# A second inner Strassen product (P4) in layer 1 of a two-layer graph attention kernel

## The chip, the cores and the metric

One core of one Trainium2 chip runs the whole program. The metric is device time in microseconds (us) of one execution. The kernel before takes 3223.03 us, the median of 3 runs (3222.26 to 3223.73). Every run here was in the fast state (granted TensorE clock 0.997 to 0.999 on the average). Chips and jobs differ by some microseconds (the medians of the kernel before lie between 3218.35 and 3221.52 us in the jobs below), so each kernel was timed in the same rounds as the kernel before.

Engines are named as in the profile: PE is TensorE, PEld its weight loads, DVE VectorE, ACT ScalarE, POOL GpSimd, SP SyncE, SPq the transfers that SyncE issued.

## The reference, cut to what matters

128 graphs of 128 nodes with 512 features go through two attention layers of 8 heads. Everything is fp32.

```python
# layer 0
Q, K, V = x @ W_q + b_q, x @ W_k + b_k, x @ W_v + b_v          # per graph 128x512 @ 512x512
attn = softmax(Q K^T / 8 + gate bias + log(adj + 1e-9));  x = attn V + x
# layer 1
q, k, v = x @ Wq.T + bq, x @ Wk.T + bk, x @ Wv.T + bv
attn = softmax(q k^T / 8 + log(clip(adj, 1e-8)));  out = (attn v) @ Wo.T + bo
x = layer_norm(x + out) * gamma + beta
```

## The kernel before

Four graphs make a group: 32 groups of layer 0 (t = 0 to 31), then 32 of layer 1 (t = 32 to 63). A group has the matrices v, q, k; from the second group of layer 1 on, k is followed by o of the group before. Each matrix (512 rows of four graphs by 512x512 weights) is done by Strassen's seven products P1 to P7 of half-size blocks; P2 in turn is done by seven products of 128x128 blocks, in four phases, each phase followed by additions on the vector engine. The products are laid out in seven slots per matrix. "b" means that the piece of the *previous* matrix stands in this matrix's slot.

```python
SLOTS = ("P1", "P2.1"), ("P4 b",), ("P3 b", "P2.2"), ("P6", "P2.3"), ("P5",), ("P7", "P2.4"), ()
PHASES = {"1": ("P1", "P2", "P5"), "2": ("P6",), "3": ("P7",), "4": ("P4", "P3")}

def matmul(dst, lhsT, rhs, start, stop):          # two halves of 64 array columns side by side
    for half in HALVES:
        nc.tensor.matmul(dst[half], lhsT[:, half], rhs, start=start, stop=stop, skip_group_check=True)

def inner(phase):                                  # one phase of P2
    v = t["t1"]
    if phase == "1": out_tile(); t["c"] = bank("p1")
    p, a, b = t["c"], Strassen.inner_weight(*t["W"]), t["B"]["inner"]
    for k, j in enumerate(Strassen.PHASES[phase]):
        ... matmul(p[:, at * N : (at + 1) * N], x, y, phase == "1" and k == 0, True)
    if phase == "1":   onto(v, 0, p, C21); add(0, 0, p, v, 0, 1)      # vector engine
    elif phase == "2": onto(v, C12, p, C21)
    elif phase == "3": onto(v, 3, p, C21); add(0, 0, p, v, 3, 4, C12 - 3)
    else:              add(0, 0, p, v, 1, 3); add(1, 1, t["b"], t["u3"])
```

PSUM banks: P1, P6, P7 and P4 of a matrix share p0 or p3, by turns; P5 and P3 use p2; the inner P2 uses p1. So a matrix's P1 takes the bank that the last but one matrix used. Each engine's queue gets its instructions in the order of the program. The parts of the schedule that the argument touches (a = slot 0 of the o that follows k of t, so a + 7 is slot 0 of v of t + 1; "pre" stands ahead of the slot's products, "post" behind them):

```python
put(pre,  a + 4 + step * k, scores, t, k)          # k = 0, 1: graphs (0, 1), (2, 3); then exp and the masked multiply
put(pre,  a + 7 + step * k, mix, t, (2 * k, 2 * k + 1))        # av products
put(post, a + 7 + step * k, normalise, t, k)
put(post, a + 8 + step * k, move, t, k, ...)       # 16 small DMAs o -> aT, which transposes by 32x32 blocks
put(post, a + 15, count, t)                        # two small vector operations on 128x32 and an accumulator read
put(post, first + ... + 7 * (b // 2) * late, load_graph, n, b, nc.sync)   # 4 DMAs of xT per graph
put(post, o + stored, store, t, k)                 # GpSimd: h*gamma, +beta; then the DMA of h (two buffers)
```

## Time and profile before

| view of the kernel before | value |
|---|---|
| TensorE busy, its share of the chain that ended last | 99%, 93% |
| period of a layer-0 group, of an undisturbed layer-1 group | 43.71, 55.56 us |
| outer product, inner product, start to start | 1.727, 0.218 us |
| layer-1 waits of TensorE for the store of h, sum | 3.5 us |
| vector engine's addition of a bank and an SBUF tile, 128x128, 128x256 (means of the groups) | 0.288 to 0.292, 0.425 to 0.426 us |

The prediction shows the lines and how they are read; two habits matter below. Ends of matmuls are modelled and overlap, so distances are taken from start to start. And a group of lines such as "x16" counts the trace's records, two for each fp32 matmul: an outer product, 8 matmul halves, shows as x16.

### The profile page before, as it was taken

The page shows a single profiled execution, that of the slowest core. Times are in us where ns is not written, and L with a number is a line of the kernel's source. Part 1 is how long each engine was busy: PE and PEld are TensorE (multiplying, and loading weights), DVE is VectorE, ACT ScalarE, POOL GpSimd, SP SyncE. Part 2 cuts the span into 40 slices and gives each one's busy share as a digit, 9 for nine tenths or more (in the row PEclk, how much of TensorE's full clock was granted, in tenths as well). Part 3 has the DMA queues.
Part 4 walks back from the last instruction along what each step waited for, and adds up shares of the span by engine and source line. Part 5 has one row for each costly group of instructions (what it writes and reads, how often), then busy time and mean ns, then how long its engine had stood idle before and what let it go on. Part 6 is the DMA issues. An engine that isn't in the chain of part 4 may idle for free.

```text
span 3215.3 us, 95438 instructions
## 1 busy us (share of the span) xinstructions
PE 3192.1 (99%) x39970; PEld 2371.2 (74%) x39970; DVE 1988.4 (62%) x4075; ACT 1132.9 (35%) x1949; POOL 1826.5 (57%) x1892
## 2 busy tenths in 40 slices
PE   9999999999999999999999999999999999999998
PEld 6777777777777777777777777777777777777775
DVE  6666666666666666675565555555565555555565
ACT  2333333333333333333333333333333333333332
POOL 4434433434433434475766767676766767676775
PEclk9999999999999999999999999999999999999999
DMA  5333333333333333342434334343433334343432
GB/s 126 84 80 83 78 83 70 83 80 84 79 84 67 84 82 83 92 112 55 93 72 78 89 75 94 72 98 67 91 75 77 89 75 95 72 99 66 90 75 76
DMA packets 1017246, 265.83 MB, mean 83 GB/s; under 512 B 942704, under 2 KB 949872, under 8 KB 1016816
## 3 DMA queue, kind: packets, MB, share of 16 engines
q1 hardware_dynamic: 1015728, 258.39, 36.0%
q8 instruction: 319, 5.23, 0.7%
q10 hardware_dynamic: 832, 1.05, 0.1%
q14 instruction: 111, 0.91, 0.1%
q0 software_dynamic: 256, 0.26, 0.0%
HBM read 159.92 MB, written 67.11 MB: 71 GB/s over the span
## 4 chain that ended last, share of the span: by engine, by line
PE 93%; SPq 3%; DMA 1%; POOL 1%; DVE 1%; issue 1%; ACT 0%; DVEq 0%; POOLq 0%; ACTq 0%
PE p3v L128 10%; PE p0q L128 9%; PE p3k L128 9%; PE s L128 8%; PE av L128 7%; PE p2v L128 7%; PE p2q L128 7%; PE p2k L128 6%; PE p0o L128 6%; PE p0k L128 4%; PE p3q L128 4%; PE p0v L128 3%; SPq L128 3%; PE p2o L128 3%; PE p1q L128 3%; PE p1v L128 3%
## 5 line engine op out<-in xcount | busy, mean ns | idle before, releaser
L128 POOL TENSOR_TENSOR xn<-o,xn 128x512 f32<-128x512 f32 x128 | 151.1, 1201 | 661.2 <-DVE o L128 423.3
L128 DVE TENSOR_TENSOR e<-e,adjT 128x1024 f32<-128x1024 f32 x256 | 419.0, 1677 | 139.4 <-ACT e L128 139.4
L128 POOL TENSOR_TENSOR xn<-xn,row 128x512 f32<-128x512 f32 x256 | 361.7, 1435 | 169.9 <-DVE gw L128 138.0
L128 PE MATMUL p0q<-T,wq 128*64 128x256 f32 x2256 | 267.5, 379 | 0.0
L128 PE MATMUL p3k<-T,wk 128*64 128x256 f32 x2256 | 267.5, 379 | 0.0
L128 PE MATMUL p3v<-wv,T 128*64 128x256 f32 x2256 | 267.4, 379 | 0.0
L128 PE MATMUL s<-qT,kT 64*128 64x128 f32 x4096 | 263.1, 278 | 0.0
L128 PE MATMUL av<-v,e 128*64 128x65 f32 x8192 | 262.0, 221 | 0.0
L128 PEld LDWEIGHTS av<-v,e 128*64 128x64 f32 x8192 | 257.8, 137 | 1.0 <-issue 0.8
L128 PEld LDWEIGHTS s<-qT,kT 64*128 64x128 f32 x4096 | 238.6, 188 | 22.6 <-issue 12.1
L128 POOL TENSOR_TENSOR h<-h,gamma 128x512 f32<-128x512 f32 x122 | 156.3, 1281 | 115.0 <-ACT h L128 115.0
L128 PEld LDWEIGHTS p3k<-T,wk 128*64 128x64 f32 x2256 | 159.5, 137 | 67.4
L128 PEld LDWEIGHTS p3v<-wv,T 128*64 128x64 f32 x2256 | 159.0, 137 | 67.6
L128 PEld LDWEIGHTS p0q<-T,wq 128*64 128x64 f32 x2256 | 159.4, 137 | 67.1
L128 POOL TENSOR_TENSOR T<-xT 128x512 f32<-128x512 f32 x128 | 193.9, 1515 | 18.0 <-DVE xT L128 14.4
L128 ACT COPY o<-av 128x520 f32<-128x520 f32 x256 | 151.8, 593 | 133.2 <-PE av L128 120.8
L128 POOL TENSOR_TENSOR h<-h,xn 128x512 f32<-128x512 f32 x124 | 157.7, 1303 | 43.2 <-ACT h L128 40.4
L128 DVE SCALAR_TENSOR_TENSOR gw<-xn,gw 128x512 f32<-128x512 f32 x256 | 177.4, 693 | 4.4
L128 DVE STREAM_TRANSPOSE xT<-xT 128x512 f32<-128x512 f32 x252 | 177.1, 703 | 0.7 <-issue 0.7
L128 PE MATMUL p0o<-wo,T_o 128*64 128x256 f32 x1488 | 176.6, 379 | 0.0
L128 DVE TENSOR_TENSOR t1q<-p1q,t1q 128x128 f32<-128x128 f32 x189 | 54.5, 288 | 180.2 <-PE p1q L128 180.2
L128 POOL TENSOR_TENSOR h<-h,beta 128x512 f32<-128x512 f32 x122 | 156.5, 1283 | 9.6
(231 smaller groups left out, 6559.1 us busy)
## 6 DMA issues: line engine op xcount, KB each, us to landing
x1d<-xn SPq DMA_DIRECT2D x64, 512.0 KB, 3.0
xT<-x1d SPq DMA_DIRECT2D x512, 64.0 KB, 2.5
xn<-x1d SPq DMA_DIRECT2D x64, 512.0 KB, 6.9
xT<-in_x_dram SPq DMA_DIRECT2D x496, 64.0 KB, 2.8
xn<-in_x_dram SPq DMA_DIRECT2D x62, 512.0 KB, 4.1
aT<-o SPq DMA_DIRECT2D x984, 32.0 KB, 2.0
out_dram<-h SPq DMA_DIRECT2D x60, 512.0 KB, 4.6
adjT<-in_adj_dram SPq DMA_DIRECT2D x256, 64.0 KB, 3.7
```

The source lines that it names most:

```text
L128: return lambda *args, **kw: self.tc.keep_in_program_order(f(*args, **kw))
```

## The change: its intent, and the diff

In layer 1 after its first group, P4 is also done by seven products of 128x128 blocks, for v, q, k and o: 123 matrices. That takes 8 matmul halves of 256 columns off and adds 14 of 128. P4's bank is shared with P1/P6/P7, so its four phases are scattered over the next matrix's slots. Since k's P4 now ends only in slot 4 of o, the scores of graphs 0 and 1, which read it, move one slot later, and their av products with them. SBUF is made free by smaller buffer counts; some work moves from GpSimd to the vector engine; the end of the last group is reordered.

```diff
-    SLOTS = ("P1", "P2.1"), ("P4 b",), ("P3 b", "P2.2"), ("P6", "P2.3"), ("P5",), ("P7", "P2.4"), ()
+    SLOTS = (
+        ("P1", "P4.1 b", "P2.1"), ("P4 b",), ("P3 b", "P4.2 b", "P2.2"), ("P6", "P4.3 b", "P2.3"), ("P5", "P4.4 b"),
+        ("P7", "P2.4"), (),
+    )
+    INSIDE = {t: ("P2", "P4") if t > NG else ("P2",) if t else () for t in range(LAST)}
+    INSIDE.update({("o", t): ("P2", "P4") if t > NG else () for t in range(NG, LAST)})
...
-        def inner(phase):
-            v = t["t1"]
+        def inner(i, phase):
+            m, v = (1, t["u3"]) if i == "P4" else (0, t["t1"])
...
+            if i == "P4" and i in inside:
+                return
...
-        nc.gpsimd.tensor_scalar_add(rs, MV[t][:, bs, 1], LN_EPS)
+        nc.vector.tensor_scalar_add(rs, MV[t][:, bs, 1], LN_EPS)
...
-            put(pre, a + 4 + step * k, scores, t, k)
+            put(pre, a + 4 + L * (1 - k) + step * k, scores, t, k)
...
-                put(pre, a + 7 + step * k, mix, t, (2 * k, 2 * k + 1))
+                m = a + 7 + L * (1 - k) + step * k
+                put(pre, m, mix, t, (2 * k, 2 * k + 1))
...
-            put(post, a + 15, count, t)
+            put(post, a + 17, count, t)
...  (last group: other order, other banks, sum and total of the count apart, last stores from SyncE and ScalarE by turns)
```

## The prediction

> **What bounds the kernel now.** I read the page first: the busy row, then the chain that ended last.
>
> ```profile
> PE 3192.1 (99%) x39970; PEld 2371.2 (74%) x39970; DVE 1988.4 (62%) x4075; ACT 1132.9 (35%) x1949; POOL 1826.5 (57%) x1892
> ...
> PE 93%; SPq 3%; DMA 1%; POOL 1%; DVE 1%; issue 1%; ACT 0%; DVEq 0%; POOLq 0%; ACTq 0%
> ```
>
> TensorE is the bound: 93% of the chain is its own work, and the clock row shows full speed in every slice. So the change is worth what it takes off TensorE, less what it makes TensorE wait. Next, the timeline of TensorE for 2500 to 2512 us, in layer 1 (start, length, group):
>
> ```profile
> 2503.66 1.90 PE L128 MATMUL p0o<-wo,T_o 128*64 128x256 f32 x16
> 2505.39 0.39 PE L128 MATMUL p1o<-wo,inner_o 128*64 128x128 f32 x4
> 2505.61 0.39 PE L128 MATMUL p1o<-woi,aT 128*64 128x128 f32 x4
> 2505.83 2.04 PE L128 MATMUL av<-v,e 128*64 128x65 f32 x64
> ```
>
> Read start to start, since modelled ends overlap. An outer product (x16) takes 2505.39 - 2503.66 = 1.73 us; one product of 128x128 blocks (x4) takes 0.22 us. Over the whole trace the medians of these differences are 1.727 us (1,338 outer products) and 0.218 us. A steady layer-1 group of four matrices repeats every 55.56 us, a layer-0 group every 43.71 us.
>
> Last, the timeline of all engines for 2047 to 2053 us, the worst TensorE wait of layer 1:
>
> ```profile
> 2047.23 1.59 SPq L128 DMA_DIRECT2D out_dram<-h  x1
> ...
> 2047.68 1.90 PE L128 MATMUL p3k<-T,wk 128*64 128x256 f32 x16
> ...
> 2047.97 0.29 DVE L128 TENSOR_TENSOR t1o<-p1o,t1o 128x128 f32<-128x128 f32 x1 [1.26 <-PE p1o L128]
> ...
> 2049.41 1.90 PE L128 MATMUL p2k<-xT,wk 128*64 128x256 f32 x16
> ...
> 2051.82 0.29 DVE L128 TENSOR_TENSOR h<-p1o,t1o 128x128 f32<-128x128 f32 x1 [3.56 <-DMA out_dram<-h]
> ...
> 2052.26 0.44 PE L128 MATMUL p1o<-woi,inner_o 128*64 128x128 f32 x4 [0.95 <-POOL T_o L128]
> ```
>
> The vector engine's first write of h waits for the previous group's store of the same buffer, 3.56 us; phase 2 of the inner P2 of o comes 0.44 us after that write starts. (The page names POOL, which had ended before; the write of h fits better.) Call w that wait of h. In all 8 groups with such a TensorE wait it equals w - 2.43, for w over 2.43 (w 2.96: 0.52 us; 2.64: 0.21), 3.5 us in total. The sum of w is the longest DMA wait of the vector engine:
>
> ```profile
> DVE h L128: 43.7, 24
> ```
>
> Why is the store late? SyncE's queue issues, without a gap, 16 aT, 8 xT, 16 aT, 8 xT and then the store, 33.2 to 35.4 us in all, and the store lands some 3.6 to 5.5 us later. The chain starts 0.32 us after TensorE's last read of aT (P3 of the previous o, in slot 2 of v).
>
> [...] 0.432 us for a pair of halves of 256 columns, 0.218 for 128; half the columns cost 50.5%. [...] an inner product ahead of the scores (128*64 to 64*128) takes 0.10 us more, 60 times in layer 1. Scores still follow inner products, so this stays. [...]
>
> **The change part by part.**
>
> 1. TensorE work. In layer 1 after its first group, v, q, k (31 groups) and o (30) get P4 inside: 93 + 30 = 123 matrices. The order listing confirms 984 outer halves fewer and 1,722 inner more, 8 and 14 per matrix. Each saves 1.727 - 7 x 0.218 = 0.201 us; 123 x 0.201 = **24.7 us** off the path. A group falls to 54.76 us.
>
> 2. Vector engine. Per matrix three partial sums and three adds more (0.29 us, 0.43 for 256 columns), for o four adds. Layer 1 gets 555 128x128 additions, 120 more for o and 93 of 256 columns: 675 x 0.29 + 93 x 0.43 = 236 us, and about 20 us of small scalings that leave POOL; some 8.2 us a group. It is busy 31 of 55 us now, then about 40: not the bound. ScalarE loses about 120 copies, beside the path.
>
> 3. POOL. Eight 128x128 sums (0.46 us) more per group, about six small operations (0.2) fewer: +2.4 us on 38 of 55. Beside the path.
>
> 4. Slack. P4 leaves slot 1, which is then empty. From phase 1 to phase 2 of the inner P2 TensorE has P4 + P3 = 3.45 us now; afterwards P3 and one inner P4 product, 1.945 us. Where the vector engine only needs 0.29 + 0.29 us this is enough (v, q, k). For o it has to fit h's wait too: TensorE will wait for w' - 0.93 instead of w - 2.43.
>
> 5. How w shifts. From the end of o's P3 to the end of P2 phase 1 of the next o, adding blocks up gives 36.2 us now (measured 36.2) and 37.3 after, because two P4 end pieces move behind. That helps by 1.1. But mix of k=0 moves to slot 1 of v, right ahead of that P3. After mix ends come the two copies (0.81 us), reciprocal (0.24) and scaling (1.37), so o is ready about 2.6 us after mix; P3 ends after 1.73. So the chain of aT starts about 0.9 instead of 0.32 us after P3. Net w' = w - 1.1 + 0.6 = w - 0.5. The sum of (w - 1.49) over the 30 groups, where positive, is 15 us, against 3.5 now: **+11.5 us**. A wait delays the next chain as much as the next o, so it does not wear off.
>
> 6. End of the last group. From the last mix of k=0 to TensorE's last large product: now 1.87 + 1.83 + 24.05 us; afterwards about 25.9, as P4 is split and the transposes get other banks (two waits for ScalarE's copies there, 0.7 and 1.1 us). The vector engine's tail after it stays at about 7 us, then 6 us to the end of the program. -1.5 us, 0.2 of it counted already: **-1.3**.
>
> 7. Start. Twenty small warming products instead of four; the first real product waits for weights (8.3 us) and the next for a copy behind a DMA on the vector engine. Nothing, within 0.3 us. Smaller buffer counts in the small pool and halves of qT and kT: their readers come long before. POOL's four extra weight sums at the layer change are beside the path.
>
> Sum: 3223.0 - 24.7 + 11.5 - 1.3 = 3208.5. I say **3207**: part 5 rests on tenths of a microsecond, and the two-sided error is longer downwards.
>
> **The rivals.**
>
> A. The whole gain arrives: no new waits, and the old 3.5 us go too. 3223.0 - 24.7 - 3.5 - 1.3 = 3193.5. For it: vector engine and POOL both have over a quarter of each group left, and v, q, k have no DMA in the loop. Against it: the 24 waits of h in 30 groups, and a slack cut by 1.5 us.
>
> B. My chosen one: the store of h takes part of the gain back, at 3203 to 3215.
>
> C. The store takes nearly all: if the chain starts 1.1 us later rather than 0.6, w' = w, and 27 us of waits against 3.5 leave 3223.0 - 24.7 + 23.8 - 1.3 = 3221.
>
> D. The vector engine becomes the bound. It would need 55 us a group against 40; its in-order queue can delay an inner phase behind two masked multiplies (1.6 us each), but scores come a slot from the phases that need it. Up to 5 us; over 3225 very unlikely.
>
> **Range and chances.** A is the low end, C the high: 3195 to 3217 should hold it 8 times in 10. Two per cent are 64 us; TensorE saves 25 at most, and no wait I see costs 64. Faster 0.01, same 0.97, slower 0.02.
>
> **What would show it right or wrong.** Part 1: the p0 and p3 groups with 128x128 shapes at 0.218 us from start to start. Part 4 and 5: waits of TensorE in p1o phase 2 behind p3k's or p0k's inner product, 10 to 20 us in all, each following a vector-engine wait for out_dram<-h of over 0.9 us; group periods of 54.8 plus 0 to 2 us. If the periods are 54.8 flat, A is right and my reading of the slack is wrong. Part 5: the first aT issue about 0.9 us after o's P3. Part 6: from the last outer TensorE product to the end still some 13 us. Wrong altogether if the granted clock falls, or if vector-engine lateness shows in v, q and k as well.

## The result, and the profile after

The changed kernel took 3227.38 us, the median of 6 runs (3225.94 to 3230.91); the kernel before in the same rounds 3221.52 (3219.43 to 3223.73). The ratio is 1.0019, with a 95% interval of 1.0007 to 1.0032. Ratios here are the mean time of one kernel's fast runs over that of the other's of the same rounds, so not quite the ratio of the medians. Within 2% it is "the same", but it is slower, and the 3207 us and the range up to 3217 were wrong.

The page of the changed kernel, busy row and chain:

```profile
PE 3191.9 (99%) x41478; PEld 2455.4 (76%) x41478; DVE 2267.1 (70%) x4970; ACT 1045.2 (32%) x1764; POOL 1913.9 (59%) x1968
...
PE 86%; SPq 6%; DVE 5%; DMA 2%; issue 1%; ACT 0%; POOL 0%; DVEq 0%; POOLq 0%; ACTq 0%
```

TensorE is busy for 99% as before, which tells nothing: its ends are modelled. The chain tells more. TensorE's own work has gone from 93% to 86%; DVE, 1% before, and SyncE's transfers have come in. Layer-0 periods are unchanged at 43.71 us, so the difference is in layer 1, where the prediction had 54.76 us a group and the shortest measured is 55.54. Adding up start-to-start distances of a whole group between fixed products shows three places that are longer than their products.

**Place one: k's P1, 0.34 us late in every group.** All engines of the changed kernel, end of q and start of k (start, length, engine, line, operation, tiles, and in brackets the idle time before it):

```profile
2149.87 1.28 POOL L135 TENSOR_TENSOR h<-h,gamma 128x512 f32<-128x512 f32 x1
...
2150.23 0.39 PE L135 MATMUL p3v<-wv1i,T 128*64 128x128 f32 x4
2150.27 0.90 DVE L135 TENSOR_SCALAR rs<-mv 128x2 f32<-128x2 f32 x1
2150.45 1.90 PE L135 MATMUL p0q<-T,wq 128*64 128x256 f32 x16
2151.09 0.17 DVE L135 TENSOR_SCALAR ok<-rc 128x32 f32<-128x32 f32 x1
2151.23 1.27 POOL L135 TENSOR_TENSOR h<-h,beta 128x512 f32<-128x512 f32 x1
2151.29 1.26 DVE L135 SCALAR_TENSOR_TENSOR ok<-rc,ok 128x32 f32<-128x32 f32 x1
...
2152.39 0.39 PE L135 MATMUL p1q<-xT,wq1i 128*64 128x128 f32 x4
...
2152.48 0.41 DVE L135 TENSOR_TENSOR v<-p3v,u3v 128x256 f32<-128x256 f32 x1
...
2152.95 0.87 PE L135 MATMUL p3k<-xT,wk 128*64 128x256 f32 x6 [0.17 <-DVE v L135]
```

v's P4 is complete in bank p3 at about 2150.5. The addition that reads it (v<-p3v,u3v) starts at 2152.48, because it stands in the vector engine's queue behind rs and the two operations of the count (ok). k's P1 reuses p3 and starts 0.56 us after q's last inner product instead of 0.22. It also takes 1.78 us itself, start to start, instead of 1.727 in all 30 groups, so 0.39 us a group; the expectation of count_early below reckons 30 x 0.39 = 11.7. Two small operations are very long: 0.90 us for two columns, 1.26 us for 32. Both end as GpSimd's operation ends. The count's second operation by itself, before and after (number, then shortest, median and longest in ns):

```profile
L128 DVE SCALAR_TENSOR_TENSOR ok<-rc,ok x64: 191/192/194, 81.2 to 3206.8; 128x32 f32<-128x32 f32 x64
```

```profile
L135 DVE SCALAR_TENSOR_TENSOR ok<-rc,ok x64: 191/391/1267, 84.2 to 3216.1; 128x32 f32<-128x32 f32 x64
```

In layer 1 of the changed kernel it is long in 30 of 31 cases, and in all 30 it ends 46 to 54 ns after the GpSimd operation during which it began. rs is alike: in 31 of 66 cases it takes 0.86 to 0.97 us and ends 23 to 27 ns after GpSimd's gamma (beta once), in the others 0.15 to 0.17. The additions of a bank and an SBUF tile are not held up: of 1,830 at 128x128 in this trace 803 begin inside a 128x512 operation of GpSimd, and none is longer than 0.30 us. What sets these operations apart, no view shows. The change moved the root (rs, LN_EPS added to the variance) onto the vector engine and the count two slots later, both beside GpSimd's gamma and beta.

**Place two: from P3 of o to the scores, 0.32 to 0.49 us too long in every group.** TensorE of the changed kernel there:

```profile
2183.57 2.01 PE L135 MATMUL p2o<-wo,aT 128*64 128x256 f32 x15
2185.30 0.38 PE L135 MATMUL p0o<-woi,innerP_o 128*64 128x128 f32 x2
2185.41 0.38 PE L135 MATMUL p2o<-wo,aT 128*64 128x256 f32 x1
2185.52 0.38 PE L135 MATMUL p1v<-wv1i,innerP 128*64 128x128 f32 x2
...
2188.32 0.38 PE L135 MATMUL s<-qT,kT 64*128 64x128 f32 x2
```

P3 (p2o) has 15 records, then two of the next product, then its sixteenth: the two halves of the array have got out of step, and one runs alone at the end of the stretch. Records overtake each other: the last of p2o, ahead of p0o in the program, starts at 2185.41, p0o at 2185.30. The stretch takes 4.75 us (2183.57 to 2188.32) instead of 1.727 + 0.436 + 1.727 + 0.436 + 0.10 = 4.43. The list of instructions with their waits names a suspect, the same in both kernels:

```
p2o<-wo,aT 64x256 [waits for 8 DMAs and DVE]      first half
p2o<-wo,aT 64x256 [waits for 8 DMAs]              second half
```

Fifteen of these 17 waits become eight instructions of their own in TensorE's queue, 51 ns long and some 0.1 us apart. In the kernel before they run from 2120.11 to 2120.93 in the profile, well inside P4 of o, and P3's first two halves start at 2122.039 and 2122.046. In the changed kernel av stands ahead of P3, with matmuls 28 ns apart; the eight run from 2183.01 to 2183.83. The four of the second half come last, two of them after the first half has started, at 2183.573, and the second half starts 0.31 us later. Ahead of this stretch, in most groups, v's inner P2 also waits (0.15 us) for the vector engine, which has two masked multiplies ahead of the additions of o, since the scores come a slot later; place two is this and the halves.

**Place three: the store of h**, as predicted. Waits of the changed kernel (engine, tile, who ended the wait: sum in us, times, longest):

```profile
DVE h L135 <- DMA out_dram<-h: 28.5, 23, 2.7
...
PE p1o L135 <- DVE h L135: 8.4, 10, 1.6
```

Counted from start to start, TensorE's waits here are 11.2 us in this profile.

This profile was the slowest of the six runs (3230.91 us). A later one of the same kernel (run after_again, span 3221.0, kernel before 3215.3) serves for the sum:

| part of the span | after less before, us |
|---|---|
| start and layer 0 | -0.8 |
| first two groups of layer 1, the av that moved out of them counted in | +1.1 |
| 29 groups: P4 inside | -22.8 |
| 29 groups: old waits for the store | -3.9 |
| 29 groups: place one 11.3; P3 of o to the scores 9.9; ahead of it 5.4; store of h 3.9; other 0.4 | +30.9 |
| last group and end, without the av that moved into it | +1.1 |
| sum | +5.6 |

The spans differ by 5.7 us. P4 does bring its part; the waits take it back.

### The profile page after: what moved, and what is told of

Same layout as the page of the kernel before. It is cut to its first block, busy times and chain, and to the rows that moved or that the text cites. A ratio compares the mean times of both kernels' runs of the same rounds, so it can differ in the third digit from the quotient of the medians.

```text
span 3228.8 us, 99418 instructions
## 1 busy us (share of the span) xinstructions
PE 3191.9 (99%) x41478; PEld 2455.4 (76%) x41478; DVE 2267.1 (70%) x4970; ACT 1045.2 (32%) x1764; POOL 1913.9 (59%) x1968
## 4 chain that ended last, share of the span: by engine, by line
PE 86%; SPq 6%; DVE 5%; DMA 2%; issue 1%; ACT 0%; POOL 0%; DVEq 0%; POOLq 0%; ACTq 0%
PE p3v L135 9%; PE p3k L135 8%; PE s L135 7%; PE p0q L135 7%; PE av L135 7%; PE p2v L135 7%; SPq L135 6%; PE p2k L135 6%; PE p0o L135 6%; PE p2q L135 5%; PE p0k L135 4%; PE p3q L135 4%; PE p0v L135 3%; PE p2o L135 3%; PE p1v L135 3%; PE p1k L135 3%
## 5 line engine op out<-in xcount | busy, mean ns | idle before, releaser
L135 POOL TENSOR_TENSOR xn<-xn,row 128x512 f32<-128x512 f32 x256 | 380.1, 1505 | 132.6 <-DVE gw L135 123.9
L135 PE MATMUL p3v<-wv,T 128*64 128x256 f32 (+1 forms) x2132 | 249.5, 361 | 0.5 <-DVE u3v L135 0.5
L135 PE MATMUL p3k<-T,wk 128*64 128x256 f32 (+1 forms) x2132 | 239.9, 360 | 0.0
L135 PE MATMUL p0q<-T,wq 128*64 128x256 f32 (+1 forms) x2132 | 239.6, 360 | 0.0
L135 PEld LDWEIGHTS p3k<-T,wk 128*64 128x64 f32 x2132 | 149.0, 137 | 57.7
L135 PEld LDWEIGHTS p0q<-T,wq 128*64 128x64 f32 x2132 | 148.1, 137 | 58.5
L135 ACT ACTIVATE e<-s 128x1024 f32<-128x1024 f32 x128 | 124.3, 1022 | 125.3 <-PE s L135 125.3
L135 PE MATMUL p0o<-wo,T_o 128*64 128x256 f32 (+1 forms) x1368 | 159.0, 354 | 0.8 <-DVE u3o L135 0.4
```

The lines of the kernel that those rows point to most:

```text
L135: return lambda *args, **kw: self.tc.keep_in_program_order(f(*args, **kw))
```

## The experiments

Theory: three independent causes, each an accident of position (the count beside GpSimd, av ahead of P3's semaphores, the store behind xT in SyncE's queue). Rivals: the vector engine has too much to do, whatever its order; or the rest of the change is what costs.

| run | median us (n) | range | before, same rounds | ratio (95% interval) |
|---|---|---|---|---|
| count_early | 3220.95 (13) | 3217.3 to 3227.5 | 3218.69 | 1.0010 (1.0002 to 1.0018) |
| mix_between | 3221.79 (13) | 3212.3 to 3227.6 | 3218.69 | 1.0012 (1.0004 to 1.0021) |
| store_first | 3218.41 (13) | 3216.7 to 3220.3 | 3218.69 | 1.0001 (0.9992 to 1.0009) |
| all_but_p4 (wrong results) | 3236.67 (5) | 3234.8 to 3239.3 | 3218.69 | 1.0059 (1.0045 to 1.0072) |
| after_again | 3224.84 (16) | 3222.5 to 3228.2 | 3218.35 | 1.0022 (1.0015 to 1.0030) |
| three_mended | 3191.56 (5) | 3190.7 to 3193.0 | 3218.35 | 0.9918 (0.9904 to 0.9931) |
| three_mended_old_end (wrong results) | 3191.03 (5) | 3189.8 to 3193.2 | 3218.35 | 0.9916 (0.9903 to 0.9930) |
| before_store_first | 3216.61 (13) | 3213.1 to 3218.6 | 3218.35 | 0.9992 (0.9984 to 1.0000) |
| store_first_touch | 3231.72 (5) | 3230.1 to 3233.7 | 3219.43 | 1.0038 (1.0024 to 1.0051) |
| store_first_gamma_later | 3211.09 (9) | 3209.7 to 3212.3 | 3219.43 | 0.9976 (0.9966 to 0.9985) |
| three_mended_xt | 3189.25 (4) | 3188.9 to 3189.5 | 3219.43 | 0.9906 (0.9891 to 0.9921) |
| two_mended | 3219.59 (13) | 3210.6 to 3223.1 | 3218.91 | 1.0000 (0.9991 to 1.0008) |

**count_early**, an edit of the changed kernel:

```diff
-            put(post, a + 17, count, t)
+            put(post, a + 15, count, t)
```

> One edit to the changed kernel: the layer-1 and layer-0 count (two small vector-engine operations on 128x32) goes back from the post of q's slot 3 to that of q's slot 1. Theory: its second operation, 0.19 us in the profile of before, takes 1.26 us in that of the changed kernel because it stands beside GpSimd's multiplications for the store [...]; the addition that reads v's P4 bank is queued behind it, and the first product of k, which reuses that bank, waits 0.34 us, in all 30 groups [...]. Expected: from q's last inner product to k's P1 0.22 us instead of 0.56, period 55.3 in undisturbed groups instead of 55.65, time 3227.4 - 11.7 = 3216 us. Rival: the vector engine simply has too much to do in that slot, and taking 0.4 us of work elsewhere only moves the wait: under 3 us of gain, the 0.56 stays above 0.4.

The wait is gone: 0.22 us from q's last inner product to k's P1 in all groups, the shortest period 55.14. The count's second operation takes 0.19 us in all 31 groups. But the time falls by only about 4 us against the changed kernel (1.0010 against 1.0022), not 11.7: TensorE's waits for the store of h are 11.8 us in this profile. The mechanism holds, the expected time does not.

**mix_between**: av of graphs 0 and 1 between P1 of v and P4 of o.

```diff
-                m = a + 7 + L * (1 - k) + step * k
-                put(pre, m, mix, t, (2 * k, 2 * k + 1))
+                between = t > NG and k == 0
+                m = a + 7 + (L * (1 - k) if not between else 0) + step * k
+                put(mid if between else pre, m, mix, t, (2 * k, 2 * k + 1))   # mid: behind the slot's first product
```

> One edit to the changed kernel: in layer 1 the av products of graphs 0 and 1 go between P1 of v and the inner P4 of o, instead of right ahead of P3 of o. Theory: the semaphores that P3 of o waits on (its two halves read what 16 DMAs brought) take some 0.1 us each in TensorE's queue; during the short av products (28 ns each) the queue is not far enough ahead, the second half of the array starts one matmul late, and the stretch from P3 of o to the scores takes 4.75 to 4.92 us instead of 4.43. Expected: that stretch at 4.43, P1 of v to P3 of o at 4.91 instead of mostly 5.06, together 0.45 us a group or 13 us; the chain of aT starts about 1.3 us earlier, which takes 5 to 8 us off the waits for the store of h. Time 3206 to 3214 us. Rival: the halves get out of step because of their own operands, wherever av stands: 4.75 stays and only the 5 to 8 us are gained, 3220 us.

The halves are in step in all groups: P3 of o is one piece of 16 records everywhere. TensorE of this run:

```profile
2120.82 0.61 PE L135 MATMUL p0o<-wo,T_o 128*64 128x128 f32 x8
...
2122.14 1.90 PE L135 MATMUL p2o<-wo,aT 128*64 128x256 f32 x16
2123.86 0.39 PE L135 MATMUL p0o<-woi,innerP_o 128*64 128x128 f32 x4
...
2126.56 0.71 PE L135 MATMUL s<-qT,kT 64*128 64x128 f32 x7
```

The stretch is 4.42 us here and 4.43 in most groups; in 6 it is 4.70 to 4.90 for another reason, which is shown under two_mended. From P1 of v to P3 of o it is 4.91 throughout. The expected 5 to 8 us off the store did not come, and again most of the gain is missing. The chain of aT starts 0.16 us after the vector engine has scaled o (0.48 once), and this scaling stands behind the additions of the slot: the chain starts 0.75 to 0.96 us after P3 in most groups, 0.80 to 0.88 in most of after_again, so an earlier av does not bring it forward.

**store_first**: the second half of the loads of xT two slots later, behind the store.

```diff
-                put(post, first + (-1 if t == 0 else 2 + 7 * (b // 2) * late), load_graph, n, b, nc.sync)
+                put(post, first + (-1 if t == 0 else 2 + 9 * (b // 2) * late), load_graph, n, b, nc.sync)
```

> One edit to the changed kernel: the last eight loads of xT (graphs 2 and 3) are issued two slots later, so that the store of graphs 0 and 1 stands ahead of them in SyncE's queue and is issued about 5.4 us earlier. Theory: the vector engine's first write of h waits for this store, and TensorE for that; the sum of TensorE's waits there is about 11 us in the profile of the changed kernel. Expected: no TensorE wait left between k's inner P4 and the second phase of o's inner P2 (0.22 us each), time 3227.4 - 11 = 3216 us. Rival: the store lands late because it is long in landing and not because it is issued late, or the loads of xT become the late ones: no gain, or a new wait of GpSimd's sums and TensorE at v's first product.

The waits are gone in all 30 groups: the vector engine's first write of h starts 0.03 us after the addition ahead of it (0.16 once). All periods lie between 55.40 and 55.71, and the runs spread over 3.6 us, against 10 to 15 in the two runs above and 5.7 in after_again: the store made the periods scatter, and part of the spread between runs. The gain is 6.4 us against after_again by the medians, not 11. The stretch of place two is 0.32 to 0.39 us too long a group in this run, which has no other wait there.

**all_but_p4**: P4 done whole, every other part of the change kept. The results are wrong, because the inner weights of P4 had still been written over the plain ones; the instructions and their order are those meant.

```diff
-    INSIDE = {t: ("P2", "P4") if t > NG else ("P2",) if t else () for t in range(LAST)}
-    INSIDE.update({("o", t): ("P2", "P4") if t > NG else () for t in range(NG, LAST)})
+    INSIDE = {t: ("P2",) if t else () for t in range(LAST)}
+    INSIDE.update({("o", t): ("P2",) if t > NG else () for t in range(NG, LAST)})
```

> The changed kernel with the seven products inside P2 alone, as before (and in the o matrices too); every other part of the change stays. Theory: the three waits of the changed kernel are made by P4 lying inside (no P4 addition of v for k's bank to wait on, an outer P4 of o between av and P3), so they go, and with them the 24.7 us of saving: periods of 55.56 plus the old waits for the store, time 3221.5 plus 2 to 5 us for the last group and the start of layer 1, 3223 to 3227. Rival: the other parts (later mix, later count, roots on the vector engine) cost some 30 us by themselves and P4 inside brings its 24.7 in full: 3250 us.

Neither. The period is 56.18 us, 0.62 above before. 0.58 of it is one wait: v's inner P2 behind P1 of v (2.30 us instead of 1.73), for the vector engine's additions of o (the view of waits has PE p1v behind DVE h 29 times), which stand behind the two masked multiplies of the scores that came a slot later. So the later scores, which P4 of k forces, cost by themselves (read from the trace; no run moved them alone); with P4 inside, its first phase stands in that place and hides most of it (0.15 us left). The waits of places one and two are not there, as expected.

**after_again**, the yardstick of the second job.

> The changed kernel unaltered, on the chip and in the rounds of the runs beside it, as their yardstick. Theory: slower than the kernel before by 0.1 to 0.3 per cent, spread over 5 to 10 us by the waits for the store of h, which differ from run to run. Rival: the first measurement was an accident of that chip, and the two are equal within 0.05 per cent.

The slowdown is confirmed on another chip: 1.0022.

**three_mended**: the three edits together.

> The changed kernel with all three edits: count early, av between P1 of v and P4 of o, store ahead of the second loads of xT. Theory: the three waits are all that stood between the change and its 24.7 us in layer 1, and the first two edits alone gave little because each shortens the group and the chain of 48 issues and the store of h, whose length is fixed, takes the time back; with the store moved as well they add up. Expected: periods of 54.75 to 54.85 us in every group of layer 1, no scatter; the time is that of the store-first run, 3218.4, less 30 x (0.39 + 0.32 + 0.15) = 26: 3193 us. Rival: TensorE is then ahead of something else (loads of xT, GpSimd's sums, masked multiplications), which takes half of it back: 3203 us or more, and a new wait with a name in the profile.

All periods of the groups 35 to 62 are 54.77 us; the prediction had said 54.76. The page:

```profile
PE 3167.0 (99%) x41478; PEld 2418.7 (76%) x41478; DVE 2231.7 (70%) x4970; ACT 1046.4 (33%) x1764; POOL 1913.7 (60%) x1968
...
PE 97%; DVE 1%; SPq 1%; DMA 0%; issue 0%; POOL 0%; ACT 0%; DVEq 0%; POOLq 0%
```

TensorE's own work is 97% of the chain, with the same number of vector operations as in the changed kernel: the vector engine at 70% is not too slow, it was late. The three edits bring 33.3 us together, 3.9, 3.1 and 6.4 alone (each against after_again, by medians; the single edits ran on another chip, where the kernel before took 3218.69 us instead of 3218.35).

**two_mended**: the first two edits, the store as in the change. It asks why the parts don't add up.

> The changed kernel with the count early and av between P1 of v and P4 of o, and the store where the change has it. Theory: these two take 25 us of TensorE's waits away (30 x 0.86), but the chain of 48 issues and the store of h is not shorter, and the vector engine's wait for the store grows by about what the group shrinks between the chain's start and the next o, 0.4 to 0.8 us; so TensorE's waits there come to 8 to 20 us, and the time to 3205 to 3217 us, spread over 8 us or more between runs. Rival: the three waits are independent, and what the two edits gave singly (3.9 and 3.1 us against the changed kernel in the same job or with the same kernel before) was chance of the chip: 3199 us, like the three together plus 7, with little spread.

Waits and chain of this run:

```profile
DVE h L135 <- DMA out_dram<-h: 50.0, 28, 3.2
...
PE p1o L135 <- DVE h L135: 20.6, 20, 2.1
```

```profile
PE 80%; SPq 10%; DMA 4%; DVE 3%; issue 1%; POOL 1%; ACT 0%; DVEq 0%; POOLq 0%; ACTq 0%
```

TensorE's waits for the store come to 28.2 us, more than I expected, and the median is 2.6 us above my range. From the chain's start to the end of P2's phase 1 of the next o there are 35.9 to 36.6 us here, 35.9 in the kernel before and mostly 37.25 in after_again; the chain of issues is 33 to 36 us in all three, and the store needs some 3.5 to 5.5 more. Whatever the first two edits save in this window, the store takes. The theory holds, the independence of the waits does not.

A fourth wait is in these traces. In 13 groups of this run, and in the 6 of mix_between, the stretch from P3 of o to the scores takes 4.48 to 4.90 us although the halves are in step. All engines of this run in one of them:

```profile
1621.45 3.49 POOL L135 TENSOR_TENSOR xn<-xn,row 128x512 f32<-128x512 f32 x2
1621.65 2.15 DVE L135 TENSOR_TENSOR o<-o,rc 128x1024 f32<-128x1024 f32 x1
...
1624.33 0.27 DVE L135 TENSOR_TENSOR u3o<-p0o,u3o 128x128 f32<-128x128 f32 x1
...
1624.66 0.44 PE L135 MATMUL p0o<-wo,T_o 128*64 128x128 f32 x4
```

The scaling of o, 1.23 us at its shortest, begins inside an addition of GpSimd; in all 15 groups where it takes 1.69 us or more it ends 1.08 us after that addition. The addition u3o of the inner P4 stands behind it, and TensorE's p0o waits for u3o. This takes 3.2 us in this run and 2.2 in mix_between. It also delays the chain of aT, which starts 0.16 us after the scaling: 1.2 to 1.8 us after P3 in these 15 groups, 0.75 to 0.96 in most others. In three_mended the scaling takes 1.34 to 1.41 us in every group. No run moved GpSimd's addition alone, so this is read from the traces and not tried.

**store_first_touch**: two matmuls of one column ahead of v's inner P2 take over P3's 16 waits for DMAs; av stays ahead of P3.

```diff
+        for half in HALVES:
+            nc.tensor.matmul(p[half, 0:1], aT[:, 2, 2, half], aT[:, 2, 2, 0:1], start=True, stop=True, ...)
```

> The store-first kernel (3218.4 us) with two matmuls of one column each ahead of the inner P2 of v, which read the half of aT that P3 of o needs; av stays right ahead of P3. They take over the 16 waits for DMAs of P3 (8 on each half of the array), so P3 waits for one semaphore alone. Theory: the halves get out of step because those 16 waits stand between the first matmuls of P3's two halves, and av is too short to hide them; so without the waits the stretch from P3 of o to the scores takes 4.43 us instead of 4.75, though av has not moved: 30 x 0.32 = 10 us less, at most 0.1 us a group given back by the extra matmuls: 3208 to 3211 us. Rival: it is av ahead of P3 itself (its mixed order of halves, its waits for the masked multiplications) that puts the halves out of step: 4.75 stays, and the extra matmuls add to 3218 to 3222 us.

The halves are in step in all groups, 4.43 us, though av has not moved: the semaphores are the cause. The time is a miss: the new matmuls have the same waits and hide them no better behind inner products. They take 0.75 us a group, and P1 of v to P3 of o grows from 5.06 to 5.83 us. The waits moved, and cost more there.

**store_first_gamma_later**: the count stays in q's slot 3; ScalarE's scaling of h and GpSimd's gamma and beta come two slots later (and the loads of xT with them, behind the store).

```diff
-                    stat, scaled, end, stored = (((5, 6), 6, 9, 10), ((9, 10), 10, 13, 14))[k]
+                    stat, scaled, end, stored = (((5, 6), 6, 11, 12), ((9, 10), 10, 13, 14))[k]
```

> The store-first kernel (3218.4 us) with the count where the change put it, in q's slot 3, and the scaling of graphs 0 and 1 of h on ScalarE and their multiplication and addition on GpSimd two slots later (the loads of xT behind that store again). Theory: the count's second operation is slow (1.26 us) only because GpSimd is in a multiplication when it comes; with GpSimd at rest there it takes 0.19 us, v's addition starts on time, and k's P1 follows q's last product after 0.22 to 0.3 us instead of 0.56, with as many vector operations ahead of it as ever: 7 to 11 us less, 3207 to 3212 us. Rival: it is the number of vector operations queued ahead of that addition: 0.56 stays, time within 2 us of 3218.4.

All engines of this run, same place as in place one:

```profile
2138.97 0.17 DVE L135 TENSOR_SCALAR rs<-mv 128x2 f32<-128x2 f32 x1
2139.05 0.17 DVE L135 TENSOR_SCALAR ok<-rc 128x32 f32<-128x32 f32 x1
...
2139.26 0.20 DVE L135 SCALAR_TENSOR_TENSOR ok<-rc,ok 128x32 f32<-128x32 f32 x1
...
2139.39 0.41 DVE L135 TENSOR_TENSOR v<-p3v,u3v 128x256 f32<-128x256 f32 x1
2139.88 1.28 POOL L135 TENSOR_TENSOR h<-h,gamma 128x512 f32<-128x512 f32 x1
...
2141.02 0.39 PE L135 MATMUL p1q<-xT,wq1i 128*64 128x128 f32 x4
...
2141.24 1.25 PE L135 MATMUL p3k<-xT,wk 128*64 128x256 f32 x10
```

The same root and count stand ahead of v's addition, and take 0.17 and 0.20 us with gamma and beta out of the way. GpSimd is not quite at rest: its power of 128x2 (0.69 us in the record) begins some 0.04 us before the count's second operation in all 30 groups and does not hold it up (0.20 us in all 30). k's P1 follows after 0.22 us. It is gamma and beta, not the number of operations. Of the 11 us that place one costs, 5.0 arrive in the groups of this profile, since k's products lose 0.2 us a group elsewhere. Another 2.8 us come from the second group of layer 1 (60.8 us in store_first, 58.0 here), whose loads of xT the edit also put later; so the time of 3211 us, though in the expected range, is not place one alone.

**before_store_first**: the store edit on the kernel before.

> The kernel before with the one edit to the order of the loads of xT and the store of h. Theory: its waits for the store (3.5 us in its profile, those of 2.43 us and more of the vector engine) go, and with them most of the scatter between runs: 3 to 4 us faster than before, runs within 4 us of each other. Rival: the scatter and the waits have another source (the load of natural x, the clock): no difference over 1 us.

The profile has no store wait left (periods 55.56 and 55.57, 3.9 us less), but the time falls only by 1.7 us. In that profile the first o of layer 1 waits longer for its transposed input (3.3 us instead of 1.2), and the granted clock fell to 0.5 for 3.4 us right behind this wait: 65.2 us against 61.0 for that group. Whether the edit or that run made the wait longer was not tried apart. The runs spread over 5.5 us, not within the expected 4 (8.1 for the kernel before).

**three_mended_old_end**: the last group's end as before (wrong in four graphs, since P4 of that o is done whole with overwritten weights).

> As the run before it, and the last group's end in the order of the kernel before (its P4 of o done whole, the graphs 0 and 1 of the last group but one first, all last stores from SyncE). The results of four graphs of 128 are wrong on purpose: P4 done whole reads weights that the inner P4 has overwritten. Theory: from the first product of the last v to the end takes 97 to 98 us with the changed order and 94.5 before; some 1.5 us of the excess are the change's order on the vector engine after the last product, and the rest waits of the new order, so the old order brings 2 to 3 us: 3190 to 3191 us, the stretch 94 to 95 us. Rival: the excess is only the three waits in the last group (0.86 us) and the later scores, which stay: within 1 us of the run before.

The medians differ by 0.5 us, within both intervals. From the first product of the last v to the end the profiles have 96.5 us, 96.8 in three_mended and 94.5 in the kernel before; 94 to 95 were expected. The rival holds: going back to the old order gains next to nothing.

**three_mended_xt**: in the second group of layer 1 also, the loads of xT behind the chain of aT.

```diff
-                put(post, first + (-1 if t == 0 else 2 + 9 * (b // 2) * late), load_graph, n, b, nc.sync)
+                put(post, first + (-1 if t == 0 else 2 + (12 if t == NG + 1 else 9) * (b // 2) * late), load_graph, n, b, nc.sync)
```

> The kernel with the three edits (3191.6 us) and, in the first group of layer 1 that has one, the second eight loads of xT behind the second chain of aT. Theory: what TensorE still waits for once, 2.1 us at the first o of layer 1 (its vector addition stands behind a turn of aT that waits for its DMAs), is the issue of that chain, 5.4 us of which is xT; so the second group's period falls from 60.1 to 58 us, time 3189.5 us. Rival: the chain's landing is set by its bytes or by av, not by the issue, or GpSimd's sums become the limit: less than 0.7 us gained.

The group takes 58.01 us, as expected. This version computes the right result and is the fastest: 3189.25 us, 0.9906 of the kernel before.

## Why the prediction was wrong

- **Part 1 (24.7 us saved by TensorE)** was right. three_mended has 54.77 us a group, predicted 54.76; before_store_first 55.56, both without waits.
- **Part 2 (vector engine busy about 40 of 55 us, not the bound)** was right as a share and led to the wrong conclusion. POOL's share (**part 3**) was right as well, and it was the pair of the two that mattered.
- **Part 4 is the step that failed:** "Where the vector engine only needs 0.29 + 0.29 us this is enough (v, q, k)". It looked at one hand-over alone, from phase 1 to phase 2 of the inner P2, and counted the vector engine's two additions there, not what stands ahead of additions in its queue. The waits came at two other hand-overs. The bank of v's P4 is needed by k's P1, and the count, held up by GpSimd, made that addition 2 us late: 11.3 us. The bank of o's inner P2 is needed by v's, and the later scores put masked multiplies ahead of the additions of o: most of the 5.4 us. The prediction's own sign of being wrong altogether, "vector-engine lateness shows in v, q and k as well", came true for v. The profile of before could have warned: its masked multiply of 128x1024 took 1.21 to 2.30 us for the same work.
- **Part 5** noted that av moves "right ahead of that P3", but only asked what it does to the chain of aT. What it did to TensorE's queue, 9.9 us, is in no part and in none of the rivals. The size of the store's waits, 11.5, looks right beside 11.2 and 3.9 us in two profiles, but for a wrong reason. The waits of the vector engine average 1.77 us before, and were to shift by -0.5. In two_mended, without the lateness, they average 1.67, a shift of -0.1, and TensorE's waits come to 28.2 us: this is **rival C** (27 us). The term at fault is the chain's start after P3 of o, put at 0.9 us: it is 0.8 to 1.8 there (one 0.3), 1.28 on the average, set by the end of o's scaling on the vector engine. Where the scaling took 1.23 to 1.44 us (1.37 predicted), 0.9 was right (0.75 to 0.96 in 11 of 13 groups); what the sum lacks is the hold-up of the scaling beside GpSimd, in 15 of 29 groups. In the changed kernel the lateness gave the store 0.7 us more per group (0.39 + 0.32), and their average fell to 0.96 and 0.52. So two errors partly hid each other. (Its own figures give w - 0.5 - 0.93 = w - 1.43, not w - 1.49: 16.1 us instead of 15. And the range ended at 3217 although rival C's sum was 3221.)
- **Part 6 (-1.3 us)** was wrong, and the term that failed is the vector engine's tail, "about 7 us". From the last mix of k=0 to the end of TensorE's last large product there are 26.0 us, as predicted (25.9; before 27.75; the difference of the part's own figures is 1.85, not 1.5). With the moved av taken out, last group and end are +1.1 us. P4 inside accounts for -0.8 of that and places one and two for about +0.9, so the new order cost some 1 us instead of gaining 1.3. From the end of TensorE's last large product (start plus length below) to the vector engine's last operation there are 8.8 us, and there were 6.9. Of TensorE and of the vector engine at the end:

```profile
3195.19 7.03 PE L128 MATMUL po<-wo_plain,aT_last 128*128 128x512 f32 x16
...
3209.16 0.14 DVE L128 TENSOR_SCALAR bad<-good_total 1x1 int32<-1x1 f32 x1
```

```profile
3206.89 7.13 PE L135 MATMUL po<-wo_plain,aT_last 128*128 128x512 f32 x16 [0.24 <-ACT aT_last L135]
...
3222.80 0.14 DVE L135 TENSOR_SCALAR bad<-good_total 1x1 int32<-1x1 f32 x1
```

  The vector engine has no idle time there. It begins the last but one of the additions h_last<-po,xn 1.2 us ahead of that end (2.2 us in the kernel before), and then has two multiply-adds with beta more to do (about 0.7 us each). In the run with the old order the tail is still 8.4 us, so how much the order has to do with it stays open.
- **Part 7 (start)** was right within 0.8 us. (The records of tr_x are 0.213 us apart in the kernel before, and in the changed one, behind the twenty small products, mostly 0.109 from 6.1 us on.) The change of layer was not: in after_again TensorE waits 2.0 us at the first o of layer 1 (1.2 before), and three_mended_xt took 2 us off that group. In the first profile of the changed kernel this wait was 3.1 us, and the granted clock fell to 0.5 for 3.4 us behind it, as in before_store_first; this is part of why that run was the slowest.
- **Rival D** named the right thing, an in-order queue, and the wrong size: "Up to 5 us; over 3225 very unlikely". The vector engine's queue cost 16.7 us (11.3 and 5.4); the other 9.9 us of place two are TensorE's queue. Its reason, that scores come a slot ahead of the phases that need them, was true before the scores moved.

What decides the time is now settled: with the waits removed one by one the shortest periods come out at 55.14, 55.15, 55.63 and, together, at 54.77 us. The three causes and the coupling between them are shown by runs; the hold-up of o's scaling and the 1 us of the last group are not.

## What to carry to other kernels

When products are split into smaller ones, the waits between them grow more numerous and the slack shorter (here, by the prediction's figures, 1.945 us instead of 3.45 between two phases of the inner P2): for each bank that is reused, list what stands ahead of its reader in that engine's queue, and look for GpSimd operations beside it: here the rest of one made a 0.19 us operation take 1.26 us. Put short products neither ahead of an instruction with many semaphores nor in its place (here 0.32 to 0.39 us a group ahead of it, 0.75 in its place). And if several waits lie in one loop with a chain of fixed length, mend the chain first; otherwise it takes what the other mends give (28.2 us of TensorE's waits for the store in two_mended).
